# Separate step offsets for the first three and the last four pairs of a two-layer graph kernel

## The chip, the cores and the metric

The kernel runs on one core of a Trainium2 chip. The metric is the device time of one execution in microseconds (us). Before the change the median of three runs is 2439.91 us (2439.7 to 2441.08). One more execution was recorded by the hardware profiler; all views of the trace are of that one.

A core has five engines, each with its own instruction queue that it works off strictly in the order of the program: TensorE (PE, matrix products; PEld is its loading of the stationary operand), VectorE (DVE), ScalarE (ACT), GpSimd (POOL) and SyncE (SP, which here only issues DMA transfers). Engines wait for each other through semaphores.

## The reference: what is computed

The inputs are 128 graphs of 128 nodes with 512 features, `x` (128, 128, 512), and an integer adjacency `adj` (128, 128, 128), all in 32 bits. Two layers follow each other, each with a residual addition and a layer normalisation:

```python
# layer 0: masked attention with 8 heads of 64
q, k, v = inputs @ Wq + bq, inputs @ Wk + bk, inputs @ Wv + bv     # split in heads
logits = einsum('bqhd,bkhd->bhqk', q, k) / sqrt(64)
attn = softmax(where(adj > 0, logits, -1e9))
x = layernorm(x + relu(einsum('bhqk,bkhd->bqhd', attn, v) @ Wo + bo))
# layer 1: graph attention with one head
Wh = x @ W
e = leaky_relu((Wh @ a1)[:, :, None] + (Wh @ a2)[:, None, :], 0.2)
x = layernorm(x + elu(softmax(where(adj == 0, -1e9, e)) @ Wh))
```

## The kernel before, in words

The batch is worked in 64 pairs of graphs. Each pair is a chain of about 130 small steps, from the load of x to the store, that lasts over several pairs' time, so that some eight pairs are in work at any moment. The four dense products of a pair (q and k together, v, o, w) are each done in seven block products instead of eight, by a scheme of the Strassen and Winograd kind: sums of blocks of the left side (`left_sums`: x_sums, o_sums, z_sums) and of the weight (`weight_sums`: sums_qk, sums_v, sums_o, sums_w, done once) are made first. Seven products go into three PSUM banks A, B and C (`PRODUCTS`: products 0 and 2 go to A, 1, 3 and 5 to B, 4 and 6 to C), and between two products in one bank another engine copies the partial result out. The steps that do this are, for q and k, qk_p1, qk_p1q and qk_c11 (ACT, bank A), qk_p6, qk_p7 and qk_c21 (DVE, bank B), qk_c22 and qk_c12 (DVE, bank C); for v, o and w the names are the same behind v_, o_ and w_. A product into a bank has to wait for the step that reads the bank, and each bank exists once, shared by qk, v, o and w.

The rest of a pair, in the order in which the data needs it:

- SP: load_blocks (x in a layout for transposing), load_adj, load_x (x for the residual).
- DVE: x_transpose; POOL: x_sums; PE: qk0 to qk6, v0 to v6, logits.
- POOL: fill_logits (a fill with -1e9); DVE: mask_logits, max_logits; ACT: exp_logits; DVE: sum_logits; ACT: norm_logits.
- DVE: weights_t (32 x 32 transposes); SP: weights_out and weights_in, a way through memory that completes the transposition. For the last pair, weights_t is done on PE, weights_out on DVE and ACT, and weights_in is nothing.
- PE: mix_values; ACT: mix_values_out; POOL: o_sums; PE: o0 to o6; DVE: residual0, stats0, mean0; POOL: rstd0, shift0; ACT: norm0.
- Layer 1: DVE edge_term (the layer's e, for which a is folded with W once, see below), PE edge_row, ACT edge_sums, DVE edge_leaky, edge_mask, edge_max, ACT edge_exp, DVE edges_t, SP edges_t_out and edges_t_in (for the last pair PE and ACT), PE mix_nodes, ACT mix_nodes_out, POOL z_sums, PE w0 to w6, ACT elu_exp, POOL elu_low, DVE elu_max, POOL residual1, DVE stats1 and mean1, POOL rstd1 and shift1, ACT finish, SP store.

In the last pair, what POOL does in sums, elu_low and residual1 is done on DVE. A digit behind a name is the graph of the pair (0 or 1), or, in o3 or qk4, the product; edge_term10 is the second term of graph 0.

mix_values, mix_nodes, edge_row, edges_t of the last pair, and sums_fold_t all use one PSUM bank (tag `ps`), so that each of them waits for the step that emptied it after the one before.

Once per kernel, `fold_a` (sums_fold0, sums_fold1; L201 to L211) multiplies W with the two halves of a: POOL's queue issues the load of `a_bc`, DVE does eight multiplies with an accumulator and then a small addition and a copy. sums_fold_t (PE) and sums_fold_out (ACT) spread the result over the partitions. sums_qk (L129 to L132) is four subtractions on DVE, sums_v likewise; sums_o and sums_w are on POOL.

The order of the work is written out by a plan. `PLAN` holds a moment for each step, `PERIOD` the distance between pairs. Every step of every pair becomes an event, the events are sorted, and the steps are issued in that order; so on each engine the sorted order is the order of the queue. The moments are used for nothing else. The steps that occur once belong to pair 0. The function that makes an event reads a shift from `ENDS`, which is empty before the change:

```python
    def at(key, p, fn, *args):

        shift = ENDS.get(p if p < n_pair // 2 else p - n_pair, {}).get(key, 0.0)
        events.append((p * PERIOD + PLAN[key] + shift, len(events), fn, args))
```

The set-up ahead of the events (loads of the weights on SP and ACT, the biases on POOL, the scaling of Wq on DVE, L194) isn't part of the plan. SP's set-up order is blocks of x for pair 0, Wk, adj of pair 0, Wv, x and adj of pair 1, Wo, W; ACT's queue issues Wq.

Of the kernel before, what the change touches and what calls it, by code (L numbers as in the profile page):

```python
# [16 lines left out]

PERIOD = 75.72
PLAN = dict(
    load_blocks=-145.14, x_transpose1=-53.4, x_transpose0=-35.51, sums_qk=-33.34, sums_fold1=-29.39, qk0=-27.1,  # L20
    x_sums=-23.88, qk_p1=-23.14, qk1=-22.39, fill_logits0=-21.87, qk_p1q=-21.45, qk2=-21.2, qk_c11=-20.29,
    qk_p6=-19.48, sums_v=-18.68, qk3=-17.99, load_adj=-17.97, mask=-17.48, qk_p7=-16.28, qk4=-15.67, qk5=-15.2,
    qk_c22=-12.6, qk6=-10.28, v0=-9.3, qk_c21=-4.36, qk_c12=-1.71, v_p1=-1.71, logits=0.0, fill_logits1=0.47,
    mask_logits0=2.51, max_logits0=3.23, v1=3.74, v2=5.42, v_p6=9.86, v3=10.28, mask_logits1=11.03, v_c11=11.14,
    v4=11.19, v_p7=11.39, v5=11.72, max_logits1=11.91, v_c22=12.76, exp_logits0=13.09, v6=13.11, v_c21=17.62,
    v_c12=24.79, sum_logits0=38.24, exp_logits1=39.15, sums_fold0=44.28, sum_logits1=44.73, norm_logits0=46.84,
    sums_fold_t1=51.88, sums_fold_out1=51.93, weights_t0=52.11, sums_fold_t0=54.57, norm_logits1=54.59,
    weights_t1=56.92, weights_out0=69.01, sums_fold_out0=71.24, weights_out1=72.35, weights_in0=73.55,
    mix_values0=75.07, mix_values_out0=75.62, weights_in1=76.59, mix_values1=77.67, sums_w=80.78,
    mix_values_out1=82.2, sums_o=82.43, o_sums=83.08, load_x1=83.6, fill_edges=94.56, o0=106.33, o_p1=107.8,  # L30
    o1=110.7, o_p6=113.29, o4=114.99, o3=115.54, o_p1l=115.68, o_p7=116.85, o2=117.07, o5=117.95, load_x0=119.48,
    o_c11=123.99, o_c22=124.53, o6=125.56, o_c21=125.62, residual01=129.31, o_c12=132.6, stats01=134.5,
    mean01=136.37, rstd01=136.65, shift01=136.91, residual00=138.02, stats00=142.08, mean00=142.88, norm01=143.34,
    rstd00=143.95, shift00=146.71, edge_term01=147.04, edge_term11=147.54, norm00=147.98, edge_term10=152.41,
    edge_term00=152.98, edge_row=160.06, edge_sums=163.14, edge_leaky=163.47, edge_mask=167.08, edge_max=171.62,
    edge_exp=173.19, edges_t=179.68, edges_t_out=188.05, edges_t_in=199.52, mix_nodes1=209.13,
    mix_nodes_out1=213.74, mix_nodes0=214.15, mix_nodes_out0=221.07, z_sums=225.48, w0=238.82, w_p1=240.45,
    w1=248.86, w2=249.67, w_p6=251.97, w3=255.0, w_c11=255.99, w_p7=256.03, w4=256.11, w_c22=259.18, w5=259.7,
    w6=259.92, edge_norm=261.55, w_c21=261.61, w_c12=264.14, elu_exp1=276.85, elu_low1=281.16, elu_exp0=304.17,
    elu_low0=304.34, elu_max0=329.44, elu_max1=330.72, residual10=333.57, stats10=338.98, mean10=339.98,  # L40
    residual11=340.94, rstd10=361.09, shift10=363.8, stats11=376.92, mean11=380.35, rstd11=388.98, shift11=391.45,
    finish0=399.29, store0=407.37, finish1=407.57, store1=460.65)

ENDS = {}

BUFS = dict(
    xb=2, adj=4, xT=2, sx=1, e1a512=1, e1b512=1, u2512=1, pr=2, mask=1, u3512=1, qT=2, kT=2, e1a256=2, t=2, scr=1,
# [5 lines left out]
def tile_two_graph_layers(ctx: ExitStack, tc: tile.TileContext, x, adj, wq, bq, wk, bk, wv, bv, wo, bo, w, a, out,  # L53
# [34 lines left out]
    MV, RSTD, NMAX, TOT, BL, SUMS, ST = ({} for _ in range(7))  # L88
# [149 lines left out]
    def rows_product(blk, weight, left, j):  # L238

        bank, a_i, b_i = PRODUCTS[j]  # L240
        first = bank not in blk.bank
        out = blk.psum(bank)
        for c in range(2):
            nc.tensor.matmul(out, left_block(left, blk.pair, a_i, c), weight[:, b_i, c, :], start=first and c == 0,  # L244
                             stop=j in LAST and c == 1, skip_group_check=True)

    def columns_product(blk, weight, left, j):

        bank, a_i, b_i = PRODUCTS[j]
        first = bank not in blk.bank  # L250
        out = blk.psum(bank)
        for f in range(NC):
            for c in range(2):

                nc.tensor.matmul(out[:, f * P:(f + 1) * P], weight[:, b_i, c, f * P:(f + 1) * P],  # L255
                                 left_block(left, blk.pair, a_i, c),
                                 start=first and f == 0 and c == 0,
                                 stop=j in LAST and f == NC - 1 and c == 1, skip_group_check=True)
# [31 lines left out]
        left_sums("x", p, XT)  # L290

    def qk_product(p, j):
        if j == 0:
            BL["qk", p] = Blocks("qk", p, D)
        columns_product(BL["qk", p], wqk, "x", j)

# [42 lines left out]

    def half_product(tag, p, j):  # L340

        if j == 0:
            BL[tag, p] = Blocks(tag, p, HALF)
        weight, left = dict(v=(wv_b, "x"), o=(wo_b, "o"), w=(w_b, "z"))[tag]
        rows_product(BL[tag, p], weight, left, j)
# [272 lines left out]
# [5 lines that stand above are left out]
    for p in range(n_pair):  # L623
# [11 lines left out]
        for j in range(7):  # L635
            at(f"qk{j}", p, qk_product, p, j)
        for fn in (qk_p1, qk_p1q, qk_p6, qk_c11, qk_p7, qk_c22, qk_c21, qk_c12):
            at(fn.__name__, p, fn, p)
        for tag in "vow":
            for j in range(7):  # L640
                at(f"{tag}{j}", p, half_product, tag, p, j)
            for fn in (half_p1, half_p6, half_c11, half_p7, half_c22, half_c21, half_c12):
                at(f"{tag}_{fn.__name__[5:]}", p, fn, tag, p)
# [50 lines left out]
```

## Time and profile before

| What | us |
|---|---|
| median of 3 runs | 2439.91 |
| profiled execution, own time | 2441.85 |
| its span | 2440.1 |
| PE busy | 2383.7 (98%) |
| DVE busy | 1881.5 (77%) |
| ACT busy | 1570.9 (64%) |
| POOL busy | 1497.0 (61%) |
| first matmul starts | 10.46 |
| last matmuls start | 2426.96 |

The profiled execution's own time is 1.94 us above the median of the runs. Times in the trace count from the span's start. A row of the timeline gives the start, the duration, the engine, the line, the operation with output and inputs, and, in brackets, how long the engine was idle before it and what ended the idle time. The mean share of the DMA engines is 40.4% for the queue that moves nearly everything.

PE's busy time in the first 20 us is 4.69, in the next 20 it is 6.25, with granted clocks of 0.93 and 0.59 of full speed; from 120 on it is 20 of 20. From 2360 on, in steps of 20 us, it is 19.32, 15.69, 14.78 and 7.16, with clocks of 1.00, 0.83, 0.83 and 0.76.

### The profile page before, as it was taken

How to read it: one execution, taken by the hardware profiler on the slowest of the kernel's cores; microseconds unless marked ns; L12 is line 12 of the kernel's file. 1: busy time of each engine (PE TensorE's matmuls, PEld its weight loads, DVE VectorE, ACT ScalarE, POOL GpSimd, SP SyncE). 2: the span in 40 equal slices, each digit the busy share in tenths (PEclk: the TensorE clock that was granted, in tenths of full speed). 3: DMA queues.
4: the chain of work that ended last, by engine and by line, in shares of the span. 5: the costliest groups of instructions: out<-in, count | busy, mean ns of one | idle time of the engine just before them, and what ended most of it. 6: DMA issues, size and time to landing. Idle time of an engine off the chain costs nothing. (4 is left out here: it accounts for less than half of the span.)

```text
span 2440.1 us, 51873 instructions
## 1 busy us (share of the span) xinstructions
PE 2383.7 (98%) x17818; PEld 2156.8 (88%) x17818; DVE 1881.5 (77%) x3838; ACT 1570.9 (64%) x5510; POOL 1497.0 (61%) x1989
## 2 busy tenths in 40 slices
PE   4999999999999999999999999999999999999996
PEld 4899899899899998998998998998998989989985
DVE  4777877877877877877778778778778778778786
ACT  2666666667667666666666666666666676676674
POOL 1445665666666666666666656656656666666657
PEclk8999999999999999999999999999999999999998
DMA  5443443443443443443443444434434434434421
GB/s 130 113 107 101 108 120 104 114 120 97 118 123 92 118 126 93 115 121 101 112 118 99 120 113 104 120 108 110 120 100 115 122 92 119 127 92 116 121 82 53
DMA packets 305766, 267.14 MB, mean 109 GB/s; under 512 B 89760, under 2 KB 255392, under 8 KB 305504
## 3 DMA queue, kind: packets, MB, share of 16 engines
q1 hardware_dynamic: 304528, 261.98, 40.4%
q8 instruction: 143, 2.34, 0.4%
q10 hardware_dynamic: 640, 1.05, 0.2%
q14 instruction: 119, 0.97, 0.1%
q0 software_dynamic: 336, 0.79, 0.1%
HBM read 155.85 MB, written 107.87 MB: 108 GB/s over the span
## 5 line engine op out<-in xcount | busy, mean ns | idle before, releaser
L425 ACT ACTIVATE pr<-pr,nmax 128x128 f32<-128x128 f32 x1024 | 394.9, 393 | 0.0
L434 ACT ACTIVATE pr<-pr,tot 128x128 f32<-128x128 f32 x1024 | 314.6, 412 | 106.6 <-DVE tot L429 106.6
L271 POOL TENSOR_SCALAR rstd<-mv 128x1 f32<-128x1 f32 x256 | 112.0, 437 | 319.7 <-DVE mv L268 310.2
L604 POOL TENSOR_TENSOR cw<-cw,co 128x512 f32<-128x512 f32 x126 | 184.3, 1482 | 163.2 <-DVE cw L601 163.2
L255 PE MATMUL pBqk<-sx,wqk 128*128 128x128 f32 x2048 | 253.1, 277 | 18.6 <-issue 13.7
L255 PEld LDWEIGHTS pBqk<-sx,wqk 128*128 128x128 f32 x2048 | 247.0, 194 | 22.1 <-issue 18.9
L255 PE MATMUL pAqk<-xT,wqk 128*128 128x128 f32 x2048 | 251.9, 277 | 13.2 <-DVE xT L286 10.5
L598 POOL TENSOR_SCALAR t<-t 128x512 f32<-128x512 f32 x126 | 245.4, 1948 | 31.5 <-ACT t L594 31.5
L279 ACT ACTIVATE co<-co,nmean,rstd 128x512 f32<-128x512 f32 x128 | 104.2, 814 | 246.8 <-DVE kT L330 216.8
L255 PEld LDWEIGHTS pAqk<-xT,wqk 128*128 128x128 f32 x2048 | 245.8, 193 | 17.2 <-DVE xT L286 10.5
L255 PE MATMUL pCqk<-sx,wqk 128*128 128x128 f32 x2048 | 250.6, 276 | 0.0
L255 PEld LDWEIGHTS pCqk<-sx,wqk 128*128 128x128 f32 x2048 | 240.0, 193 | 0.0
L484 ACT ACTIVATE oT<-po,bv 128x128 f32<-128x128 f32 x512 | 146.3, 368 | 123.2 <-PE po L475 123.2
L506 DVE SCALAR_TENSOR_TENSOR scr<-co,wa_bc 128x512 f32<-128x512 f32 x256 | 201.8, 788 | 8.4 <-ACT co L279 3.2
L425 ACT ACTIVATION_READ_ACCUMULATOR pr<-pr,nmax 128x1 f32 x1024 | 198.1, 193 | 0.0
L444 DVE STREAM_TRANSPOSE prb<-pr 128x1024 f32<-128x1024 f32 x126 | 156.2, 1239 | 49.4 <-ACT pr L434 49.4
L410 POOL MEMSET pr<- 128x1024 f32 x128 | 121.6, 951 | 99.8 <-DVE prb L444 99.8
L414 DVE COPY_PREDICATED pr<-mask,s 128x1024 f32<-128x1024 int32 x128 | 173.1, 1352 | 4.3 <-PE s L402 4.2
L272 POOL TENSOR_TENSOR rstd<-rstd,half 128x1 f32<-128x1 f32 x256 | 159.5, 623 | 21.3
L419 DVE TENSOR_REDUCE nmax<-pr 128x8 f32<-128x1024 f32 x128 | 155.4, 1214 | 2.2
L314 DVE TENSOR_TENSOR u2qk<-pBqk,e1aqk 128x512 f32<-128x512 f32 x64 | 44.2, 690 | 144.3 <-PE pBqk L255 141.6
L150 POOL TENSOR_TENSOR sx<-sx,xT 128x256 f32<-128x256 f32 x63 | 46.1, 732 | 175.6 <-DVE xT L286 175.5
(155 smaller groups left out, 6144.1 us busy)
## 6 DMA issues: line engine op xcount, KB each, us to landing
prd<-prb SPq DMA_DIRECT2D x126, 512.0 KB, 2.9
prT<-prd SPq DMA_DIRECT2D x504, 128.0 KB, 3.6
xb<-in_x_dram SPq DMA_DIRECT2D x256, 128.0 KB, 4.3
x<-in_x_dram SPq DMA_DIRECT2D x128, 256.0 KB, 3.7
out_dram<-cw SPq DMA_DIRECT2D x128, 256.0 KB, 2.0
adj<-in_adj_dram SPq DMA_DIRECT2D x64, 128.0 KB, 2.3
atd<-atb SPq DMA_DIRECT2D x63, 128.0 KB, 1.8
attT<-atd SPq DMA_DIRECT2D x252, 32.0 KB, 1.9
```

The source lines that it names most:

```text
L255: nc.tensor.matmul(out[:, f * P:(f + 1) * P], weight[:, b_i, c, f * P:(f + 1) * P], left_block(left, blk.pair, a_i, c), start=first and f ...
L272: nc.gpsimd.tensor_tensor(RSTD[key], RSTD[key], half, op=ALU.pow)
L410: nc.gpsimd.memset(PR[b], NEG)
L414: nc.vector.copy_predicated(PR[b], MASK[p][:, i, :].unsqueeze(1).to_broadcast([P, H, P]), ST.pop(("s", b)).rearrange("p j h k -> p (j h) k"))
L419: nc.vector.tensor_reduce(NMAX[b], PR[b], AX.X, ALU.max, negate=True)
L425: nc.scalar.activation(PR[b][:, h, :], PR[b][:, h, :], AF.Exp, bias=nmax[:, h:h + 1], scale=1.0, accum_out=TOT[b][:, h:h + 1])
L434: nc.scalar.activation(PR[b][:, h, :], PR[b][:, h, :], AF.Copy, scale=tot[:, h:h + 1])
L444: nc.vector.transpose(PRB[b].rearrange("p k h s -> p h k s"), PR.pop(b).rearrange("p h (k r) -> p h k r", r=32))
L484: nc.scalar.activation(OT[b][:, f, :], po[:, f, :], AF.Identity, bias=bv_sb[:, f:f + 1], scale=1.0)
L506: nc.vector.scalar_tensor_tensor(scr, X1[b], 1.0, wa_bc[s], op0=ALU.mult, op1=ALU.mult, accum_out=store[p][:, i:i + 1])
L598: side_engine(b // 2).tensor_scalar(t, t, 1.0, -1.0, op0=ALU.min, op1=ALU.add)
L604: side_engine(b // 2).tensor_tensor(Y[b], Y[b], X1.pop(b), op=ALU.add)
```

## The change

`PLAN` gets other moments for ten steps that occur once (the sums of weights and the fold of a), and `ENDS` gets seven tables of shifts, for pairs 0, 1, 2 and for the last four (-4 is pair 60, -1 is pair 63). The shifts are for the steps of that pair alone; pairs 3 to 59 keep their moments. Since products can now come in another order (qk4 ahead of qk2, for instance), two functions that opened a group of banks at product 0 open it at whichever product comes first. No instruction is added or removed.

```diff
 PLAN = dict(
-    load_blocks=-145.14, x_transpose1=-53.4, x_transpose0=-35.51, sums_qk=-33.34, sums_fold1=-29.39, qk0=-27.1,
-    ... sums_v=-18.68, ... sums_fold0=44.28, ... sums_fold_t1=51.88, sums_fold_out1=51.93, ... sums_fold_t0=54.57,
-    ... sums_fold_out0=71.24, ... sums_w=80.78, ... sums_o=82.43, ...
+    load_blocks=-145.14, sums_qk=-119.43, sums_v=-95.14, sums_fold1=-78.79, x_transpose1=-53.4, x_transpose0=-35.51,
+    ... sums_fold_t1=-3.37, ... sums_fold0=7.68, ... sums_fold_out1=17.15, ... sums_fold_t0=46.78,
+    ... sums_fold_out0=49.2, sums_o=50.12, ... sums_w=62.38, ...
-ENDS = {}
+ENDS = {
+    0: dict(
+        fill_edges=-283.56, load_adj=-90.6, qk1=-90.35, x_sums=-89.84, fill_logits0=-86.59, qk0=-85.77, mask=-85.37,
+        qk_p1=-85.08, qk4=-84.4, v2=-82.51, qk_p6=-82.46, v0=-80.61, qk_p1q=-80.24, x_transpose0=-80.05, qk3=-78.97,
+        v_p1=-77.05, qk_p7=-76.48, qk_c11=-75.7, qk2=-75.2, qk5=-74.84, qk_c22=-74.11, qk6=-72.18, v_c11=-71.65,
+        logits=-70.35, qk_c12=-70.08, qk_c21=-66.49, x_transpose1=-65.63, v1=-62.99, v4=-56.86, mask_logits0=-53.54,
+        ...
+    -1: dict(
+        load_adj=-51.23, load_x0=-50.78, edge_norm=-46.88, elu_max1=-26.6, elu_exp0=-26.2, stats11=-24.33,
+        ...
+        o5=22.54, load_blocks=33.05, weights_in0=42.11, finish0=52.85, rstd11=66.31, shift11=75.99, finish1=78.37,
+        edges_t_out=109.23, store0=137.6, store1=153.96),
+}
     def qk_product(p, j):
-        if j == 0:
+        if ("qk", p) not in BL:
             BL["qk", p] = Blocks("qk", p, D)
     def half_product(tag, p, j):
-        if j == 0:
+        if (tag, p) not in BL:
             BL[tag, p] = Blocks(tag, p, HALF)
```

In the built program the two orders differ as follows.

| Engine | start, before | start, after |
|---|---|---|
| PE | qk0 to qk6, v0, logits, v1 to v6, qk0 of pair 1, sums_fold_t1, qk1, qk2, sums_fold_t0, qk3 to qk6, v0, mix_values0, logits | qk0, qk1, qk4, qk3, qk2, qk5, v0, qk6, v2, logits, v1, v4, v3, v5, v6, sums_fold_t1, then of pair 1 qk0, qk1, qk4, qk2, qk3, v0, qk5, sums_fold_t0, qk6, mix_values0, logits |
| DVE | (scaling) x_transpose1 and 0, (scaling) sums_qk, sums_fold1, qk_p6, sums_v, mask, qk_p7, qk_c22, qk_c21, qk_c12 | (both scalings) sums_qk, x_transpose1 and 0, mask, qk_p6, sums_v, qk_p7, qk_c22, sums_fold1, qk_c12, qk_c21 |
| ACT | exp_logits0 and 1, norm_logits0, sums_fold_out1, then of pair 1 qk_p1, qk_p1q, norm_logits1, qk_c11 | exp_logits0 and 1, qk_p1 of pair 1, norm_logits0, qk_p1q, sums_fold_out1, norm_logits1, qk_c11 |
| POOL | load of a_bc, x_sums, fill_logits0 and 1, load of a_bc; later sums_w, sums_o, o_sums, fill_edges | fill_edges, x_sums, fill_logits0, load of a_bc, fill_logits1, load of a_bc; later sums_o, sums_w, o_sums |
| SP | load_blocks of 2, weights_out0 and 1, weights_in0 and 1; load_adj of 2 after two load_x | load_blocks of 2, load_adj of 2, weights_out0 and 1, weights_in0 and 1 |

| Engine | end, before | end, after |
|---|---|---|
| PE | o6 of 62, weights_t0 and 1 of 63, mix_nodes1 and 0 of 61, mix_values0 and 1 of 63, edge_row of 62, w0 to w4 of 61, o0 of 63, w5, w6, the rest of o of 63, mix_nodes1 and 0 of 62, edge_row of 63, w0 to w3 of 62, edges_t, w4 to w6, mix_nodes1 and 0 of 63, w of 63 | o6 of 62, mix_nodes1 of 61, weights_t0 of 63, mix_nodes0, weights_t1, mix_values0 of 63, w0 of 61, mix_values1 of 63, w1, w2, edge_row of 62, w3 to w6, o of 63, mix_nodes1 and 0 of 62, w0, w2, edge_row of 63, w1, w4, w3, edges_t, w5, mix_nodes1 of 63, w6, mix_nodes0, w of 63 |
| ACT | norm_logits0 of 63, elu_exp1 of 60, norm_logits1; near the end mix_nodes_out1 and 0 of 63, elu_exp0 of 62 | elu_exp1 of 60, norm_logits1, norm_logits0; near the end mix_nodes_out1 of 63, elu_exp1 of 62, mix_nodes_out0 |

Pairs 60 to 62 have their products permuted in a smaller measure, within the same stretch of work.

## The prediction, made before the changed kernel was run

> **What bounds the kernel now.** I read the page's busy rows and slices first, then busy time by window, then PE's timeline at both ends, and last the DVE rows beside PE's gaps.
>
> ```profile
> span 2440.1 us, 51873 instructions
> PE   4999999999999999999999999999999999999996
> PEclk8999999999999999999999999999999999999998
> 200.00:2200.00 2000.00, 1999.82 (x15056) 1812.94 (x15056) 1567.98 (x3193) 1323.64 (x4652) 1261.35 (x1677) 1.00 0.42 111
> ```
>
> (The last line's columns: window, its length, busy us of PE, PEld, DVE, ACT and POOL, granted clock, DMA share, GB/s.) Between 200 and 2200 us PE is busy for 1999.82 of 2000 us at full clock, so PE sets the pace there. That stretch keeps its order, and a shift at its start reaches its end unchanged. Only the ends can give time: first matmuls at 10.46, gaps until about 85, gaps from 2377 on, and 12 us after the last matmul.
>
> ```profile
> 10.46 3.56 PE L255 MATMUL pAqk<-xT,wqk 128*128 128x128 f32 x16 [10.46 <-DVE xT L286]
> 18.86 3.76 PE L255 MATMUL pBqk<-sx,wqk 128*128 128x128 f32 x16 [4.84 <-DVE wqk L130]
> 38.82 3.75 PE L255 MATMUL pBqk<-sx,wqk 128*128 128x128 f32 x16 [13.75 <-issue]
> 42.36 2.91 PE L255 MATMUL pCqk<-sx,wqk 128*128 128x128 f32 x16
> 45.10 1.95 PE L255 MATMUL pBqk<-xT,wqk 128*128 128x128 f32 x16
> 46.89 1.95 PE L255 MATMUL pCqk<-sx,wqk 128*128 128x128 f32 x16
> 49.64 2.06 PE L402 MATMUL s<-kT,qT 64*128 64x128 f32 x32
> 59.41 2.02 PE L255 MATMUL pAqk<-xT,wqk 128*128 128x128 f32 x16 [1.29 <-ACT pr L425]
> ...
> 31.87 0.42 DVE L207 SCALAR_TENSOR_TENSOR wa_scr<-w,a_bc 128x256 f32<-128x256 f32 x1 [10.88 <-DMA w<-in_L_gnn_W_dram]
> 36.09 0.43 DVE L207 SCALAR_TENSOR_TENSOR wa_scr<-w,a_bc 128x256 f32<-128x256 f32 x1 [1.36 <-DMA w<-in_L_gnn_W_dram]
> 38.03 0.68 DVE L314 TENSOR_TENSOR u2qk<-pBqk,e1aqk 128x512 f32<-128x512 f32 x1
> ```
>
> The reader is to see the large gap: PE stops at 25.07 and resumes at 38.82, and what it needs is the DVE addition u2qk (it empties bank B), which stands in DVE's queue behind the fold of a (sums_fold1, L207), which waits for slices of w until 36.09. The columns also give PE's price of a qk product: successive starts are 1.79 apart when warm (45.10 to 46.89), but 3.54 and 2.74 for the first two after a pause (38.82, 42.36, 45.10).
>
> ```profile
> 2386.92 0.69 PE L515 MATMUL pj<-ident,e 128*128 128x128 f32 x2 [1.24 <-ACT oT L484]
> 2389.11 1.91 PE L244 MATMUL pBw<-w,sz 128*128 128x256 f32 x4
> 2402.38 1.05 PE L580 MATMUL pz<-attT,co 128*128 128x128 f32 x8
> 2409.08 0.69 PE L515 MATMUL pj<-ident,e 128*128 128x128 f32 x2 [3.76 <-DVE scr L506]
> 2421.26 1.13 PE L244 MATMUL pAw<-w,zT 128*128 128x256 f32 x4 [0.68 <-ACT zT L585]
> 2426.96 1.03 PE L244 MATMUL pCw<-w,sz 128*128 128x256 f32 x4
> ```
>
> The tail is a chain: o of pair 63 ends (2402.4), residual, norm and edge terms reach edge_row (2409.08), edge softmax and mix_nodes reach w0 (2421.26), seven w products (2426.96), then 12.1 us of elu, residual, statistics and store.
>
> **The change, the first pairs.** DVE, start. Today the x transposes run at 9.11, between the two scalings of wqk. They now stand behind sums_qk (four DVE subtractions, 1.14 apart). Those wait for Wk: L130 began at 17.49, L132 at 19.77. So the transposes run 20.9 to 22.2 (1.30 for two) and PE starts at 22.3, a loss of 11.8 us. Nothing covers it.
>
> PE then runs on: qk0 22.3, qk1 25.8, qk4 28.6, qk3 30.4, qk2 32.2, qk5 33.9, v0 35.7, qk6 36.6, v2 38.4, end 39.3 (0.9 for a v product). The evacuations must keep up. u2qk follows qk1 (28.8 to 29.5), sums_v takes 4 x 0.65 (to 32.1; wv has landed, for SP issued the last wv slice by 22.1 and its median landing is 2.9), u3 33.0, kT (qk_c22) 33.7. ACT empties bank A in 2 x 1.1 us after qk0 and 1.1 after qk2, ahead of v0. All this is off PE's path.
>
> sums_fold1 comes next on DVE: eight multiplies of 0.42 and eight accumulator reads at 0.47 a couple, an add and a copy, 4.3 us, so 33.7 to 38.0. The last slices of w cap it at the same 38.03 as today, since SP's setup order is untouched. Behind it wait qk_c12 (after qk6, 38.6 to 39.3) and qk_c21 (39.9), so logits of pair 0 start at 39.6 against 49.64: 10.0 us, and v2 (0.9) is already done, 10.9. This is the core: the same fold wait, with PE work in front of it instead of behind it.
>
> The fold's a_bc load is new on that path. It is issued on POOL's queue after x_sums (four at 0.7, 21.6 to 24.4) and one fill (0.95), so at about 25.4 where it was 4.74; its two loads took 4.8 to 6.7 us to land. It arrives at 30.2 to 32.1, at least 1.6 us before the fold; I take nothing. SBUF, section "SBUF: two separate sides", of the Trainium skill speaks against this: a load from POOL's queue can starve while DVE holds the port they share, with 620 ns becoming about 3100 as its example. By it a_bc could land some 2.5 us later, an estimate from that page, and the gain would be 1 us less; sums_v runs just then. No row shows it.
>
> To saturation: mask_logits, maxima and v evacuations (1.33, 1.21, 0.41 each, in the new order) put the transposes of pair 1 at 46.9 to 48.2, so its qk0 starts at 48.3 with sums_fold_t1 (0.45) done, against 59.41: 11.5 ahead. I then find three waits against today's 1.43 at qk2: qk_p1q now stands behind norm_logits0 (2.44) on ACT, so qk2 waits 1.3; v0 waits 0.5 for qk_c11 behind norm_logits1; and mix_values0, since weights_in0 on SP is queued behind weights_out1 (its prb is done at 59.1; issue 59.6, the four loads out by 61.8, landing median 3.6), waits 0.8. The mix_values0 that began at 75.52 begins at 64.8: 10.7. sums_o and sums_w swap on POOL (8 x 1.25, from 60.5 behind a fill that waits for weights_t1, to 70.6) and o_sums give so by 72.1, ahead of o1 at 74.8. load_adj of pair 2, fill_edges (0.31 on an idle POOL) and earlier x loads have free buffers and cost nothing. Head: **-10.8**, ends -12.3 (none of those waits, pauses as warm as allowed) and -7.5 (each wait twice as long).
>
> **The change, the last pairs.** Up to o6 of pair 62 the same products are permuted; some adjacent pairs get closer (qk6 to logits has one product between instead of two), which I price at 0 to 1 us by the 0.2 to 0.6 us waits that evacuations cost elsewhere. Then PE's order is mix_nodes1 of 61, weights_t0 of 63, mix_nodes0, weights_t1, mix_values0, w0, mix_values1, w1, w2, edge_row of 62, w3 to w6, and all of o of 63 after that. All these transposed results share one PSUM bank; today they follow each other and PE waits 0.68, 1.38, 1.68, 1.24 for ACT to empty it, then runs three w products at 1.71 instead of 0.87. With 1.9 us transposes and w products between them, I add up: mix_nodes1 at 2376.1 (attT lands later, edges_t being seven places down on DVE), transposes 2377.0 and 2379.9 (norm_logits1 is before norm_logits0 on ACT now, done 2376.3), mix_values 2381.9 and 2384.4, edge_row 2387.1, w6 to 2390.9, o of 63 to 2397.2 against 2402.4: 5.2.
>
> Behind that is the chain. DVE and POOL do residual, statistics, rstd and shift for two batches in the old 6.7 us, edge_row could go at 2403.9. But w0 and w2 of pair 62 now stand before it, w0 waits for zT (2401.9), and w2 for w_p1 on ACT, queued behind norm00. After short gaps PE is slow in the rows above, so they take 1.7 each: edge_row at 2406, only 3 ahead. Then w_p6 on DVE stands before edge_max but one interleaving w product fewer stands before edges_t and mix_nodes1 goes before w6 instead of after it; elu_exp1 (0.72) now separates the two zT copies, so w0 of 63 starts near 2416.5, 4.7 ahead. w takes 6.9 (w3 and w5 wait 0.7 and 0.8 for w_p6, w_p7 behind statistics and elu_max), last matmul 2423.2 against 2428.0. The finish has six ACT applications of 0.81 and the same POOL powers, and ends 4.5 early. Tail: **-4.5**, ends -8.7 (all 5.0 of those gaps, the 3.76, no loss) and +1 (the chain as today, plus the closer products).
>
> TensorE: Matmul & The Clock Gate, Part 1, of the Trainium skill would have the clock drop only after an idle window of some 3.4 us. The rows differ: after gaps no longer than 1.68 the w products at 2387.4 to 2392.5 came at 1.71. By the page w0 and w2 would be warm and the tail gain 1.7 more; I use the row.
>
> Sum: the profiled execution took 2441.85 (span 2440.1); 2441.85 - 10.8 - 4.5 = 2426.5. The median of the runs is 1.94 lower, 2439.91, which gives **2424.6**.
>
> **The rivals.** (1) The tail gives nothing, because the chain from o of 63 to the store is latency and the products put before edge_row cost what the filled gaps save: 2439.9 - 10.8 = 2429.1. For it: three of its links are DVE or POOL steps that stay. (2) The tail fills all gaps: 2439.9 - 10.8 - 8.7 = 2420.4. Against it: w2 before edge_row. (3) The head keeps half of its gain, since the softmax of pair 0 no longer hides beside the fold and each of my three waits triples (2.6 becomes 7.8): 2429.8. (4) Slower: the fold in front of qk_c12 and qk_c21 becomes the longer wait, because a_bc or w lands late. Each us past 38.0 moves logits by one; at a fold end of 53.3 head and tail gains are gone, and at 58.2 the kernel is 0.2% slower. That needs the fold to start at 53.9, with a_bc 28.5 us on its way where 6.7 was the longest, so it is unlikely. That the order is not what the plan says is excluded: the built program has it.
>
> **Chances.** Forecast 0.63 (own range 2421 to 2428), (1) 0.15, (2) 0.10, (3) 0.08, (4) 0.04. The range, 2420 to 2430, leaves out the slower case and the outer part of the others. About 0.2%, 4.9 us, is what a measurement of this kernel tells from none. Faster 0.95, same 0.02 and slower 0.03 follow, as only (4), and a head and tail both at their bad ends, fall short.
>
> **What would show it.** First matmul at 22.3, one slow start, no 13.75 gap, logits at 39.6, DVE's fold ending at 38.0 with qk_c12 right behind, mix_values0 at 64.8; 1999.8 busy of 2000 in the middle; near the end no gap over 1.3 before o of 63, edge_row of 63 some 29.5 us before the end (31.0 today). Wrong would be: wa_scr waiting for a_bc, new PE waits in pairs 1 and 2 above 3 us together, or the last matmul further than 17 us from the end (12.1 now).

## The result and the profile after

The changed kernel takes 2423.75 us (median of four runs, 2422.51 to 2424.71), the kernel before, run beside it, 2440.49: 0.9931 of the time, 95% interval 0.9914 to 0.9948. The prediction was 2424.6. The execution that was profiled took 2424.71, with a span of 2422.9.

The page of the changed kernel, its slices, and the window of the steady stretch (columns as in the prediction):

```profile
span 2422.9 us, 51874 instructions
...
PE   5999999999999999999999999999999999999996
...
PEclk9999999999999999999999999999999999999999
...
200.00:2200.00 2000.00, 1999.82 (x15073) 1812.22 (x15073) 1568.74 (x3193) 1323.44 (x4650) 1266.89 (x1683) 1.00 0.42 112
```

The middle is what it was, 1999.82 us busy of 2000, and PE, DVE, ACT and POOL have as many instructions as before. What was gained lies at the two ends: the first digit of PE's slices rose and the last one stayed, and the granted clock is now at 90% or more of full speed in all 40 slices.

PE's timeline at the start, and DVE's beside it:

```profile
22.01 3.39 PE L410 MATMUL pAqk<-xT,wqk 128*128 128x128 f32 x16 [22.01 <-DMA wv<-in_L_gnn_Wv_dram]
25.23 1.95 PE L410 MATMUL pBqk<-sx,wqk 128*128 128x128 f32 x16
...
39.92 2.06 PE L557 MATMUL s<-kT,qT 64*128 64x128 f32 x32 [2.07 <-DVE kT L493]
...
48.71 2.02 PE L410 MATMUL pAqk<-xT,wqk 128*128 128x128 f32 x16 [0.46 <-ACT pr L580]
...
55.37 2.05 PE L410 MATMUL pAqk<-xT,wqk 128*128 128x128 f32 x16 [1.06 <-ACT e1bqk L454]
...
65.32 1.09 PE L630 MATMUL po<-prT,cv 128*64 128x128 f32 x16 [0.97 <-DMA prT<-prd]
...
33.62 0.42 DVE L362 SCALAR_TENSOR_TENSOR wa_scr<-w,a_bc 128x256 f32<-128x256 f32 x1 [1.41 <-DMA w<-in_L_gnn_W_dram]
...
37.24 0.43 DVE L362 SCALAR_TENSOR_TENSOR wa_scr<-w,a_bc 128x256 f32<-128x256 f32 x1 [1.11 <-DMA w<-in_L_gnn_W_dram]
...
39.18 0.68 DVE L493 TENSOR_TENSOR kT<-pCqk,u2qk 128x512 f32<-128x512 f32 x1
```

The gap of 13.75 us is gone. PE begins later (22.01 instead of 10.46) and then doesn't stop until the logits of pair 0, which wait 2.07 us for kT and start at 39.92 instead of 49.64. DVE shows why they wait: the fold waits for slices of W, 1.41 us at its first multiply and 1.11 at its sixth, until 37.24, and kT comes behind the fold.

The end of PE's timeline:

```profile
2371.89 1.10 PE L630 MATMUL po<-prT,cv 128*64 128x128 f32 x16 [1.02 <-ACT zT L740]
...
2391.78 1.13 PE L399 MATMUL pAw<-w,zT 128*128 128x256 f32 x4 [0.80 <-ACT zT L740]
2393.37 1.13 PE L399 MATMUL pAw<-w,zT 128*128 128x256 f32 x4 [0.46 <-ACT e1aw L510]
2394.34 0.38 PE L670 MATMUL pj<-ident,e 128*128 128x128 f32 x2
2394.56 1.06 PE L399 MATMUL pBw<-w,sz 128*128 128x256 f32 x4
...
2403.97 1.13 PE L399 MATMUL pAw<-w,zT 128*128 128x256 f32 x4 [0.68 <-ACT zT L740]
...
2409.42 1.03 PE L399 MATMUL pCw<-w,sz 128*128 128x256 f32 x4
```

No gap over 1.3 us is left in this stretch, the w products come 0.86 to 0.97 us apart where no wait stands between, and edge_row of pair 63 (2394.34) has no wait, where it had 3.76.

To compare traces I cut each execution in three at steps that all have: the start of the logits of pair 0; one mix_values of a middle pair, which starts at 1208.05 in the trace of before; and the start of the last product. The orders between the second and the stretch of the last four pairs are the same in all kernels.

| Kernel | time | logits of pair 0 | from there to the middle | middle to last product |
|---|---|---|---|---|
| before | 2440.49 | 49.64 | 1158.41 | 1218.91 |
| after | 2423.75 | 39.92 | 1159.05 | 1210.45 |
| e1 first pairs alone | 2430.16 | 38.55 | 1158.44 | 1218.40 |
| e2 last pairs alone | 2433.06 | 48.42 | 1158.42 | 1210.90 |
| e3 edges of 1 and 2 unshifted | 2422.43 | 39.48 | 1158.79 | |
| e4 fold first | 2434.63 | 50.50 | 1158.18 | |
| e5 x transposes first | 2426.45 | 40.03 | 1160.60 | |
| e6 fold late | 2436.32 | 38.71 | 1172.11 | |
| e7 both | 2428.28 | 33.04 | 1169.83 | |
| e8 load of a early | 2424.04 | 39.33 | 1158.96 | |
| e9 w behind edge_row | 2426.45 | 38.36 | 1158.99 | 1213.81 |
| e10 interleaving alone | 2442.37 | 47.33 | 1158.43 | 1220.64 |
| e11 the same, sums kept | 2439.62 | 48.00 | 1158.41 | 1218.20 |
| e12 e3, e5, e8, fold late, sums_w later | 2419.26 | 34.27 | 1159.61 | 1210.10 |

The times of before beside the runs were 2440.49 (after), 2440.95 (e1 to e4), 2438.76 (e5 to e8, a single run), 2440.63 (e9, e10) and 2440.32 (e11, e12). Kernels with the head of before (before, e2, e10, e11) differ by 2.3 us in their first column of the trace and by 0.02 in the second: the set-up varies from execution to execution, and with this head what follows doesn't. The three traces of the new head (after, e1, e9) differ by 1.6 us in the first column and by 0.61 in the second. A head is therefore compared by its logits over several traces: 48.35 on the mean before, 38.94 with the new head (after, e1, e9), so 9.4 us earlier; then 0.0 to 0.6 are lost on the way to the middle. The end gains 8.46 at the last product, and gives 0.34 back behind it (12.45 us from the end of the last product to the end of the span, instead of 12.11).

### The profile page after: what moved, and what is told of

Its sections match the earlier page's. It is cut to its first block, busy times and chain, and to the rows that moved or that the text cites. A ratio compares the mean times of both kernels' runs of the same rounds, so it can differ in the third digit from the quotient of the medians.

```text
span 2422.9 us, 51874 instructions
## 1 busy us (share of the span) xinstructions
PE 2375.8 (98%) x17818; PEld 2149.0 (89%) x17818; DVE 1880.9 (78%) x3838; ACT 1570.4 (65%) x5510; POOL 1488.1 (61%) x1989
## 3 DMA queue, kind: packets, MB, share of 16 engines
q10 hardware_dynamic: 640, 1.05, 0.2%
## 4 chain that ended last, share of the span: by engine, by line
PE 95%; DMA 1%; ACT 1%; DVE 1%; POOL 1%; SPq 1%; issue 0%; ACTq 0%; POOLq 0%; DVEq 0%
PE pBqk L410 14%; PE pAqk L410 9%; PE pCqk L410 9%; PE pBv L399 7%; PE pBw L399 7%; PE pBo L399 7%; PE po L630 5%; PE s L557 5%; PE pz L735 5%; PE pAo L399 5%; PE pAv L399 4%; PE pCo L399 4%; PE pCw L399 4%; PE pCv L399 4%; PE pAw L399 4%; PE pj L670 1%
## 5 line engine op out<-in xcount | busy, mean ns | idle before, releaser
L753 POOL TENSOR_SCALAR t<-t 128x512 f32<-128x512 f32 x126 | 246.6, 1958 | 39.3 <-ACT t L749 39.3
```

What stands on the lines that cost most here:

```text
L753: side_engine(b // 2).tensor_scalar(t, t, 1.0, -1.0, op0=ALU.min, op1=ALU.add)
```

## The experiments

**Each end alone.** e1 keeps the new `PLAN` and the tables of pairs 0, 1 and 2; e2 keeps only the tables of the last four and the old `PLAN`.

```diff
 # e1
-    -4: dict(...), -3: dict(...), -2: dict(...), -1: dict(...),
 # e2
-    0: dict(...), 1: dict(...), 2: dict(...),
```

> The new moments and the shifts of pairs 0, 1 and 2 alone; the last four pairs as before. Theory (the two ends are independent, and the same PE steps of the middle begin 9.06 us earlier after the change than before it): 2440 - 9.1 = 2431, with the last matmul 12.1 us ahead of the span's end as before. Rival by the prediction's own sum (first pairs 10.8, last pairs 4.5): 2429.2. A second rival, that the ends depend on each other (the phase in which the last pairs arrive): more than 2 us away from 2431.

> The shifts of the last four pairs alone; start as before. Theory of independent ends: 17.2 - 9.06 = 8.1 us faster than before, so 2432. Rival by the prediction's sum: 4.5 us, 2435.5.

e1 took 2430.16 (ratio to before 0.9955, 0.9941 to 0.9970), e2 2433.06 (0.9968, 0.9956 to 0.9980), against 2440.95 for before on their chip: 10.8 and 7.9 us. Their sum, 18.7, is 2 us more than the whole change gave, within the width of the intervals; the table shows no coupling between the ends, since e1 has the last column of before (0.5 less) and e2 the second of before. The tail is worth far more than my 4.5.

**The core of the head: where the fold stands.** e4 puts sums_fold1 in front of qk_p6, where it stood, and leaves all else.

```diff
-    ... sums_fold1=-78.79, ...
+    ... sums_fold1=-102.5, ...
```

> The changed kernel with one step moved: sums_fold1 stands in front of qk_p6 of pair 0 on DVE again, all else as changed. Theory (the gain at the start is this one order: PE's products in front of the fold's wait instead of behind it): the fold ends near 39 as now, u2qk follows, PE stops after qk0, qk1 and qk4 at about 28.8 and resumes at about 40, logits of pair 0 at 51 to 52 instead of 39.9, and the time is 10 to 12 us longer, 2434 to 2436. Rival (PE's late start at 22.0 in one unbroken run is what counts, or fewer slow products): within 4 us of 2423.7.

One run, 2434.63. PE's timeline of e4:

```profile
27.80 1.95 PE L404 MATMUL pCqk<-sx,wqk 128*128 128x128 f32 x16
39.22 3.75 PE L404 MATMUL pBqk<-sx,wqk 128*128 128x128 f32 x16 [9.47 <-issue]
42.77 2.50 PE L404 MATMUL pAqk<-xT,wqk 128*128 128x128 f32 x16
```

The gap is back (9.47 us), with two slow products behind it, and the logits are at 50.50: 10.9 us of time for one step of DVE moved in front of four others. This is the mechanism that the prediction named: the same wait, with PE's work in front of it instead of behind it.

**Whether the start can be earlier.** e5 puts the x transposes back in front of sums_qk. In e6 the fold comes after qk_c12 of pair 1 (with sums_fold_t1 and sums_fold_out1 after it); e7 has both edits.

```diff
 # e5 and e7
-    ... sums_qk=-119.43, ...
+    ... sums_qk=-115.0, ...
 # e6 and e7
-    ... sums_fold1=-78.79, ... sums_fold_t1=-3.37, ... sums_fold_out1=17.15, ...
+    ... sums_fold1=64.0, ... sums_fold_t1=90.0, ... sums_fold_out1=97.0, ...
```

> The changed kernel with one step moved: sums_qk stands behind the two x transposes of pair 0 on DVE, as before the change. Theory: PE's first product goes back to about 10.5, yet the time does not change (2423.7 within 1), because logits of pair 0 are held by the fold (ends at 39.2) and not by PE; the 11.8 us of later start that the change paid cost nothing. Rival: the earlier start is passed on, and logits come up to 5 us earlier, 2419 to 2421.

> The changed kernel with sums_fold1 behind qk_c12 of pair 1 on DVE (its transpose and copy later still). Theory: without the fold in front, logits of pair 0 follow PE's products at 38.0 instead of 39.9, 1.9 us earlier; the fold's 4.4 us then stand where DVE waits 2.5 us for logits of pair 1 and cost about 1.5 to 2 us there: 2423 to 2424, no clear change. Rival: the fold is hidden in its new place and the 1.9 us stay: 2421.8.

> Transposes ahead of sums_qk, and the fold behind qk_c12 of pair 1. Theory: start and fold are two caps in a row, each hides the other, so that only both moves together free time: PE begins at 10.5, sums_qk allows the second product at 18.5, logits of pair 0 at about 33.7 instead of 39.9, less the 2 us that the fold costs in its new place: 2419 to 2420. Rival: another cap lies just behind (Wv landing for sums_v, or the softmax of pair 0 on ACT), and the time stays above 2422.

e5: 2426.45, e6: 2436.32, e7: 2428.28, one run each. In e6 and e7 the fold reads W after sums_w has replaced a block of it, so that part of the computation is another one; the instructions are the same. PE's timeline of e5:

```profile
32.49 1.03 PE L393 MATMUL pAv<-wv,xT 128*128 128x256 f32 x4
40.03 3.79 PE L551 MATMUL s<-kT,qT 64*128 64x128 f32 x32 [6.51 <-DVE kT L487]
```

In e5 PE is through with v2 by 33.4 and then waits 6.51 us for kT, which is behind the fold: the earlier start is lost at the next wait, the logits behind the pause are slow (3.79 us for 2.06), and the span of this one run is 1.7 us longer than that of after. So PE's products and the fold end at nearly the same moment in the changed kernel, and neither helps alone (e6, with the fold out of the way, has its logits at 38.71, where the new head has 38.94 on the mean). In e7 both are out of the way and the logits start at 33.04; the time doesn't show it. DVE's, POOL's and PE's timelines of e7:

```profile
57.42 0.69 DVE L488 TENSOR_TENSOR kT<-pCqk,u2qk 128x512 f32<-128x512 f32 x1 [1.53 <-PE pCqk L405]
66.43 0.43 DVE L357 SCALAR_TENSOR_TENSOR wa_scr<-w,a_bc 128x256 f32<-128x256 f32 x1 [8.32 <-DMA a_bc<-in_L_gnn_a_dram]
...
63.05 0.56 POOL L351 DMA_DIRECT2D a_bc<-in_L_gnn_a_dram  x1
...
73.58 2.08 PE L394 MATMUL pBv<-wv,sx 128*128 128x256 f32 x4 [8.52 <-DVE u2v L514]
```

A step that moves takes its DMA with it: the load of a_bc is the fold's first instruction, on POOL's queue, and there it now stood behind the eight instructions of sums_o and sums_w. DVE waits 8.32 us for it with the masks of pair 1 queued behind, and PE 8.52 for u2v; in e6 PE waits 8.76 us at the same place. None of the expectations on record had that: the rival for e7 has its time, but with other causes.

**Whether the load of a limits the fold.** e8 issues both a_bc loads in the set-up.

```diff
+    for i in (1, 0):
+        A_BC[i] = buf([P, D], F32, "t", f"a_bc{i}")
+        nc.gpsimd.dma_start(A_BC[i], ...)
     def fold_a(i):
-        a_bc = buf([P, D], F32, "t", f"a_bc{i}")
-        nc.gpsimd.dma_start(a_bc, ...)
+        a_bc = A_BC.pop(i)
```

> The changed kernel, with the two loads of a issued ahead of all steps on POOL, where one of them stood before, instead of at 25.2 and 26.6. Theory: these two loads, which now run beside the loads of Wo and W, are why W arrived later (the fold's sixth multiply began at 37.24 where it was 36.09 before); the fold ends 1.1 us earlier, at 38.0, logits at 38.8, and the time is 1 us less. Rival: W arrives late for another reason (its place behind Wo on SP's queue, whose issues shift from run to run): the sixth multiply stays at 37 or later.

One run, 2424.04, the time of after. DVE's timeline of e8:

```profile
33.68 0.41 DVE L358 SCALAR_TENSOR_TENSOR wa_scr<-w,a_bc 128x256 f32<-128x256 f32 x1
...
38.57 0.69 DVE L489 TENSOR_TENSOR kT<-pCqk,u2qk 128x512 f32<-128x512 f32 x1 [0.54 <-PE pCqk L406]
```

The fold runs through without a wait, and kT then waits 0.54 for PE: here PE, which began at 23.00, is the later one. But e1 and e9, with a_bc where the change has it, also have their logits without a wait or with 0.20, so where the load stands doesn't by itself decide when the fold ends. What was late in the trace of after was W, and why is not settled. SP took 5.88 us there (from 28.00) to issue the eight slices, and 4.98 to 5.89 in all six traces that issue a load of a_bc at about 25 (after, e1, e3, e4, e6, e9); where both loads come before 16 it took 3.75 or 3.76 (4.58 in e7, whose second load comes much later). So a load of a_bc beside those of W goes with a slower issue of W. But the fold doesn't follow the issue: in e9, with 5.89, it waits 0.86 in all, and in e5, with 3.76, its sixth multiply waits until 37.34.

**The edge chains of pairs 1 and 2.** In after PE waits 0.83 and 0.22 us for attT of pairs 1 and 2 (at 153.69 and 185.06), which before didn't have. e3 drops the shifts of the edge steps and mix_nodes of these pairs.

```diff
     1: dict(
-        edge_*=..., edges_t*=..., mix_nodes*=...,
     2: dict(
-        edge_*=..., edges_t*=..., mix_nodes*=...,
```

> The changed kernel, but the steps of the edge softmax (edge_term to edges_t_in) and mix_nodes of pairs 1 and 2 keep their old moments. Theory: the 11.1 us that PE is ahead at mix_values0 of pair 2 shrink to 9.06 because mix_nodes1 of pairs 1 and 2 waits for attT, whose edge chain now stands later in DVE's queue; without those shifts PE keeps 11 us and the time is 2 us less, 2421.7, with no PE wait for attT between 140 and 200. Rival: the waits only move to another step of these pairs (the v or o evacuations that now stand behind the edge steps on DVE) and the time stays at 2423.7.

2422.43 (ratio to before 0.9923, 0.9907 to 0.9940; that of after was 0.9931). The waits for attT are gone, but two others came, 0.26 for kT (126.47) and 0.53 for e1bqk (225.83), and from the logits to the middle the trace is only 0.26 us shorter than after. My theory that these chains cost 1.9 us is not borne out; the medians differ by 1.3 with overlapping ranges.

**The two w products in front of edge_row.** e9 puts w0, w_p1 and w2 of pair 62 behind edge_row and edge_sums of pair 63.

```diff
     -2: dict(
-        ... w0=-2.7, ... w2=-11.13, ... w_p1=-4.22, ...
+        ... w0=5.54, ... w2=-4.31, ... w_p1=4.41, ...
```

> The changed kernel, with w0 and w2 of pair 62 behind edge_row of pair 63 on PE (and w_p1 behind edge_sums on ACT) instead of ahead of it. By the prediction's reading (they hold edge_row back by 2 us): 1 to 2 us faster. By the reading of the changed trace: edge_row would begin at most 0.5 us earlier, since its last input, the edge term of graph 0, ends at 2393.86 and edge_row begins at 2394.34; edge_sums waits for one more edge term anyway; and PE stands idle for 3 us ahead of edge_row, so that the products behind it run at 1.7 instead of 0.9: the same to 2 us slower.

One run, 2426.45. PE's timeline of e9:

```profile
2392.65 0.69 PE L664 MATMUL pj<-ident,e 128*128 128x128 f32 x2 [2.80 <-DVE scr L655]
2393.13 1.92 PE L393 MATMUL pAw<-w,zT 128*128 128x256 f32 x4
2395.51 2.07 PE L393 MATMUL pAw<-w,zT 128*128 128x256 f32 x4 [0.46 <-ACT e1aw L504]
2397.37 1.46 PE L393 MATMUL pBw<-w,sz 128*128 128x256 f32 x4
```

On a common clock (e9 is 1.62 us ahead of after in the middle) edge_row starts at the same moment in both, 2394.27 and 2394.34. The two products in front of it thus cost nothing: without them PE waits 2.80 us for the edge terms instead. Behind it they come slow, and the way to the last product is 3.36 us longer than in after. The granted clock (third figure from the end) shows the difference in the same window of the two traces, first after, then e9:

```profile
2392.00:2396.00 4.00, 3.54 (x17) 2.77 (x17) 3.50 (x8) 1.80 (x4) 3.92 (x5) 1.00 0.00 0
...
2392.00:2396.00 4.00, 2.89 (x7) 1.99 (x8) 3.80 (x8) 1.00 (x3) 3.92 (x5) 0.50 0.00 0
```

So this step is one of the sources of the gain, where I had it as a loss.

**Filling the gaps alone.** e10 takes the kernel before and moves only the w family of pair 61 with z_sums and elu_max0 of the same pair, and weights_t of pair 63. e11 leaves z_sums and elu_max0 where they were. On PE this gives the order of the change from mix_nodes1 of 61 to o of 63 except in one place: w0 stands in front of mix_values0 and not behind it, so that the two mix_values still follow each other.

```diff
+    -3: dict(w1=-19.1, ... w6=-7.2, w_c12=-4.87, z_sums=-4.08, elu_max0=2.67),   # e11: without the last two
+    -1: dict(weights_t0=7.25, weights_t1=11.6),
```

> The kernel before, with only these steps of the end moved as the change moves them: w0 to w6 of pair 61 with their evacuations, z_sums and elu_max0 of 61, and weights_t0 and weights_t1 of pair 63; so the products that share one PSUM bank alternate with others, and all of w of 61 comes ahead of o of 63. Theory: this is most of the gain at the end: the four waits of 5.0 us and the slow products behind them (2.6 us) go, o of 63 ends about 6 us earlier than before, and the time is 5 to 6.5 us less, 2434 to 2435. Rival: the gain at the end comes from the later chain (edge_row, edges_t and mix_nodes of 63 among w of 62), and this alone gives under 3 us.

> The kernel before with only the last pairs' w family of pair 61 and the two weights_t of pair 63 moved, as in e10, but with z_sums and elu_max0 of pair 61 left where they were. In e10 the four z_sums (3.8 us on POOL, from 2378.58 to 2382.3) stood in front of the second nmean, so the second norm on ACT ran at 2382.72, prT was copied at 2383.44 and mix_values' result at 2384.17, and PE waited 3.70 us for oT; after it the products were slow again (1.65 and 2.08). Theory: that one step is why e10 gained nothing; without it the second gap falls from 3.70 to under 0.5, o of pair 63 is through some 4 to 6 us earlier after the steady part than in the kernel before, and the time is 2434.5 to 2437. Rival: the orders of DVE and ACT around norm and weights are needed as well, another wait takes the place of the 3.70, and the time is 2439 to 2441 as in e10.

e10: 2442.37 (1.0008, 0.9999 to 1.0018). PE's, POOL's and ACT's timelines of e10:

```profile
2379.52 1.13 PE L250 MATMUL pAw<-w,zT 128*128 128x256 f32 x4 [2.06 <-ACT zT L591]
...
2385.37 1.65 PE L481 MATMUL po<-prT,cv 128*64 128x128 f32 x16 [3.70 <-ACT oT L490]
...
2378.58 1.23 POOL L155 TENSOR_TENSOR sz<-zT 128x256 f32<-128x256 f32 x1
...
2382.42 0.26 POOL L282 TENSOR_SCALAR nmean<-mv,rstd 128x1 f32<-128x1 f32 x1
...
2382.72 0.81 ACT L285 ACTIVATE co<-co,nmean,rstd 128x512 f32<-128x512 f32 x1 [3.25 <-POOL nmean L282]
```

z_sums (L155 and three more) stood in POOL's queue in front of the second nmean, ACT's norm waited 3.25 us for that, and the copies that empty the shared bank stand behind the norm. e11: 2439.62 (0.9998, 0.9989 to 1.0008). PE's timeline of e11, and two windows of it (the third figure from the end is the granted clock):

```profile
2380.14 1.99 PE L250 MATMUL pAw<-w,zT 128*128 128x256 f32 x4 [2.04 <-ACT zT L591]
2382.06 1.87 PE L481 MATMUL po<-prT,cv 128*64 128x128 f32 x16
2385.17 1.09 PE L481 MATMUL po<-prT,cv 128*64 128x128 f32 x16 [1.24 <-ACT oT L490]
...
2389.52 1.10 PE L250 MATMUL pBw<-w,sz 128*128 128x256 f32 x4 [1.11 <-POOL at L525]
...
2380.00:2384.00 4.00, 3.78 (x20) 2.66 (x20) 3.73 (x9) 1.82 (x5) 3.92 (x4) 0.57 0.01 4
2384.00:2394.00 10.00, 7.72 (x47) 6.50 (x48) 5.33 (x13) 6.05 (x18) 4.03 (x7) 1.00 0.07 27
```

The 3.70 is gone, as expected, but 2.04, 1.24 and 1.11 are left, slow products with them, and o of pair 63 ends only 0.36 us earlier than before, counted from the middle: the rival was right. The 1.24 lies between the two mix_values that follow each other, which the change doesn't have. The 2.04, the wait for zT, comes from ACT and POOL. Their rows in e11, and POOL's in after:

```profile
2373.29 1.95 POOL L604 TENSOR_SCALAR t<-t 128x512 f32<-128x512 f32 x1 [5.70 <-ACT t L600]
2378.32 0.81 ACT L285 ACTIVATE co<-co,nmean,rstd 128x512 f32<-128x512 f32 x1 [2.31 <-POOL nmean L282]
...
2363.70 1.95 POOL L753 TENSOR_SCALAR t<-t 128x512 f32<-128x512 f32 x1 [1.35 <-ACT t L749]
```

ACT's first norm of pair 62 stands in front of the copy of zT and waits 2.31 us for POOL, which begins its 1.95 us of elu_low of pair 60 only at 2373.29, after the start of o6 of pair 62 (2372.92), since elu_exp1 stands between the two norm_logits on ACT; in after, with elu_exp1 ahead of both, POOL begins it at 2363.70, before o6 (2365.94). So by the traces the orders of ACT and POOL are part of the gain, beside the order on PE that the prediction counted. No run has PE's order of the change with the old orders of ACT and POOL, so how much each gives was not taken apart.

**What the runs point to.** e12 is the changed kernel with e5's transposes, e6's late fold, e8's early loads, sums_w behind o_sums of pair 0, and e3's edges.

```diff
-    ... sums_qk=-119.43, ... sums_fold1=-78.79, ... sums_fold_t1=-3.37, ... sums_fold_out1=17.15, ... sums_w=62.38, ...
+    ... sums_qk=-115.0, ... sums_fold1=64.0, ... sums_fold_t1=90.0, ... sums_fold_out1=97.0, ... sums_w=90.5, ...
     # a_bc as in e8, pairs 1 and 2 as in e3
```

> The changed kernel with the four things that the other runs point to: the x transposes in front of sums_qk, sums_fold1 behind qk_c12 of pair 1, both a_bc loads issued in the set-up and sums_w behind o_sums of pair 0, and the edge chains of pairs 1 and 2 unshifted. In e7 the logits of pair 0 stood at 33.0 instead of 39.9, but DVE then waited 8.32 us for a_bc, which POOL issued at 63.05 behind sums_w, and PE waited 8.5 for it. Theory: with a_bc there, the fold runs from about 58 to 62.5 in DVE's idle time, PE waits some 1 us for the masks of pair 1 instead of 8.5, 5.5 to 7 us of the logits' 6.9 are kept and the edges give 0.7 to 1.3 more: 2416 to 2418.5. Rival: the fold's 4.3 us lie on DVE's path into pair 1 wherever it stands, or o_sums and sums_w come too late on POOL: 2421 to 2424.

2419.26 (four runs, 2419.2 to 2419.56; 0.9916 of before, 0.9901 to 0.9931): some 4.5 us below the changed kernel, and outside its runs' range, though less than the 5.2 to 7.7 expected. PE's and DVE's timelines of e12:

```profile
34.27 2.06 PE L548 MATMUL s<-kT,qT 64*128 64x128 f32 x32
...
43.06 2.02 PE L401 MATMUL pAqk<-xT,wqk 128*128 128x128 f32 x16 [0.90 <-ACT pr L571]
...
66.43 1.13 PE L390 MATMUL pBv<-wv,sx 128*128 128x256 f32 x4 [0.55 <-DVE u2v L510]
...
58.65 0.69 DVE L484 TENSOR_TENSOR kT<-pCqk,u2qk 128x512 f32<-128x512 f32 x1 [1.53 <-PE pCqk L401]
59.26 0.42 DVE L353 SCALAR_TENSOR_TENSOR wa_scr<-w,a_bc 128x256 f32<-128x256 f32 x1
```

The fold starts right behind kT, without a wait; the masks of pair 1 come some 2 us later than they could, and PE waits 0.55 for u2v instead of 8.52. The logits are 4.7 ahead of the mean of the new head, and 0.6 to 1.2 of it go on the way to the middle.

## Why the prediction was right, step by step

The time lies 0.85 us from the prediction, and that is closer than the working deserves; in part it is luck. Between these two traces the head gave 9.08 us where I had 10.8, and the tail 8.1 where I had 4.5, so that a shortfall and a surplus largely cancelled; the rest is the profiled execution, which stood 1.94 us above the median before and 0.96 after. The tail's error is real, as e2 alone gave 7.9. The head's is not shown: e1 alone gave 10.8 by its medians, and the start of the logits varies by up to 2.3 us between executions with the same head.

*Start of PE.* Predicted at 22.3, it was 22.01; the loss that nothing covers was right. I had two slow products and there was one, so v2 ended at 37.9 instead of 39.3, but in this trace that bought nothing, as the logits wait for the fold.

*The fold.* Predicted to end at 38.0, with logits at 39.6: in this trace W came later, the fold's end was 39.18 and the logits 39.92. That the fold keeps its place in time and only what stands in front of it changes was right, and e4 shows it: 10.9 us. The load of a_bc was at no point late, issued at 25.18 where I had 25.4.

*To saturation.* qk0 of pair 1 at 48.71 (48.3), waits at qk2 1.06 (1.3) and mix_values0 0.97 (0.8), mix_values0 at 65.32 (64.8): right. (The prediction's own terms, 11.5 ahead less 1.2 of added waits, make 10.3 at this point and not its 10.7; the trace has 10.2.) v0 didn't wait, and a v product of pair 0 did, 0.52 for u3v. The term that was off in this trace is what I took from there: 0.8 us more gain after the logits, where 0.6 were lost. I had looked at PE's order in pairs 1 and 2 and not at DVE's, where edges_t now stands 12 instructions later in pair 1 and 3 later in pair 2; the trace has 1.05 us of waits for attT, which I put down to that. But e1 has 0.83 of these and loses 0.02 us in all, and in e3 they are gone with 0.26 gained. So what makes up the 1.4 us is not settled; the traces show only small waits that change places.

*The filled gaps.* Predicted o of pair 63 to end 5.2 us earlier on the clock of before; it was 6.0. The sum was nearly right and its reason incomplete: e11 has nearly the same order on PE and 0.36 us of the gain.

*The chain behind it.* Here the term was mis-sized. I had w0 and w2 of pair 62 at 1.7 us each in front of edge_row, as a loss of 2 us; they took 0.97, after waits of 0.80 and 0.46, and stood in a wait that was there in any case. edge_row was 5.7 us ahead instead of 3, w0 of pair 63 8.2 instead of 4.7, the last product 8.5 instead of 4.8, and the end 8.1 instead of 4.5. Of the 3.7 us that the last product came earlier than predicted, 0.8 are from the gaps, 1.9 from the delay of edge_row that did not come, and 1.0 from behind it. I took the price from the rows of before, which were right for where they stood: after a stretch of 7 us in which PE was busy for 2.69. Two windows of before, with the clock as the third figure from the end:

```profile
2380.40:2387.40 7.00, 2.69 (x35) 2.19 (x35) 5.01 (x13) 5.49 (x14) 6.82 (x7) 0.89 0.00 0
2387.40:2392.50 5.10, 5.10 (x13) 4.05 (x13) 3.62 (x9) 2.48 (x8) 2.16 (x6) 0.50 0.14 51
```

The row had to be chosen by the idle time around it, not by the instruction.

*The rivals.* (1), a tail of nothing, falls by e2. (2), all gaps filled, gave 8.7 for the tail and came nearest to it; its objection, w2 before edge_row, was the error. (3) and (4) fall by the trace: the waits between qk0 of pair 1 and mix_values0 sum to 2.03 us, with 2.6 predicted and 7.8 for (3), and the fold ended 1.2 us past 38.0.

The clock. The Trainium skill's TensorE: Matmul & The Clock Gate, Part 1, lets the clock fall after an idle window of about 3.4 us. For w0 and w2 it gave the better number, and the tail it would have made, 6.2, lies nearer to 8.1. But 3.4 us of unbroken idle time are not needed here: in before the clock fell to 0.50 after four gaps of 0.68 to 1.68 us, and in e11 the products after a gap of 2.04 us, behind 1.04 us of transposes, are slow, with a clock of 0.57 over the next 4 us, while gaps of 1.24 and 1.11 us in the 10 us after that leave it at 1.00.

## What to carry to other kernels

When a step moves, list what it issues besides its arithmetic; the load at its head goes into another queue, and in e7 this cost more than the move had won. Two limits that end at nearly the same time have to be moved together: alone, the earlier transposes (e5, one run) lost 1.7 us, and with the fold, its load and sums_w moved as well, and the edge chains of e3, the kernel gained 4.5 (e12). A product put into a wait that is there anyway can be free and keep the clock up, as w0 and w2 did; price it by the idle time around its new place, not by a row from another one.

## What the runs showed of the hardware

- The set-up differs between executions of the same instructions by up to 2.3 us (logits at 47.33 to 49.64 with the old head). What lies between the logits and the middle repeated within 0.02 us over 1158 in those four traces, but only within 0.61 in the three of the new head. One trace is not enough to tell a head's gain to a microsecond.
- By the distance of the starts, the clock came up after one slow product in after (3.22 us from the first start to the second), and after two behind a pause in e12 (3.55 and 2.26) and in e4.
- Three of DVE's multiplies of the second fold took 0.73, 0.83 and 0.83 us instead of 0.42 while POOL's x_sums ran beside them (49.2 to 51.7 in after), and two of POOL's took 0.91 instead of 0.73. The Trainium skill's SBUF — State Buffer, "SBUF: two separate sides", has DVE instructions with two SBUF inputs and GpSimd instructions that read SBUF take turns at one pair of ports; these rows agree. The same section's starved loads, weighed in the prediction, didn't show: those of a_bc from POOL's queue landed in 4.3 to 5.8 us beside DVE's sums_v, no later than the 4.8 to 6.7 of before. The section tells this of DVE's two-port modes, with a float32 copy as its example; sums_v are subtractions of two inputs, so the prediction stretched it.
